# Band scores by halves of the keys, in banks that a run keeps, in a fused two-axis attention layer

## The chip, the cores and the metric

The kernel runs on one core of a Trainium2 chip. The metric is the device time of one execution in microseconds (us), lower being better. The engines of a core are named as the profile names them: PE is the matrix engine (TensorE) and PEld its weight loads, ACT is ScalarE, DVE is VectorE, POOL is GpSimd, and SP is the engine whose queue issues the DMAs. PE writes to PSUM, which has eight banks of 512 fp32 values in each of 128 partitions[...].

## The reference

The input is x of shape [2, 256, 128, 128]: batch, time T, band F, channels C. All of it is fp32. Three residual steps follow each other:

```python
xt = _ln(x, ln_t_w, ln_t_b).transpose(0, 2, 1, 3)
x = x + _mha(xt, ..., H_T, causal mask over T).transpose(0, 2, 1, 3)   # 4 heads of 32 channels
xf = _ln(x, ln_f_w, ln_f_b)
x = x + _mha(xf, ..., H_F, band mask over F)     # |i - j| <= 16 of 128 positions
xn = _ln(x, ln_n_w, ln_n_b)
x = x + (gelu(xn @ w1.T + b1) @ w2.T + b2)       # 128 -> 512 -> 128
```

`_mha` projects to queries, keys and values, takes softmax(q k / sqrt(32) + mask) v for each head, and projects back. What matters here is the second step: for each of the 512 pairs of batch and time there are 128 positions along F, and a position sees only the 33 nearest ones.

## The kernel before

The work is cut into groups of four tiles of 128 tokens (NT = 4), 512 tokens in all. There are three kinds, as classes: `OverTime` (attention along T, 128 groups), `OverBands` (attention along F, 128 groups) and `FeedForward` (128 groups). All groups of time come first; their result goes to HBM and is read back. Then runs follow: 8 groups of bands, then the 8 groups of feed-forward on the same tokens, 16 times (RUN = 32 time steps, `groups`).

`BoundedPath.run` issues the work. Each pass n of its loop issues pieces of several groups: the scores of group n, the weighing by the values of group n - 1, the output product of group n - 2, queries, keys and values of group n + 1, the normalisation of group n + 3, the statistics of groups further ahead. The order is written out by hand: the wrapper `InOrder` pins each engine's instructions to the order in which they are issued, so no scheduler moves them, and all of them carry the wrapper's line (L861) in the profile. The profile is read by the names of the tiles.

A band group goes through these pieces. `queries_keys` computes `qp` and `kp` on PE, and `take_query`, `take_key` copy them by ACT to `qT`, `kT` with channels on partitions. `values` and `take_values` do the same for `vp`, `v`. `scores` (called by `first_half`) computes for each of the 4 tiles and 4 heads the scores `sp`, keys on partitions and queries along the free dimension, a matmul of contraction 32 with 128 keys and 128 queries; every head has a bank, and each head uses its own 32 rows of PE, so four matmuls of one tile can stand side by side. `first_function` lets DVE add a band of -1e30 to the scores of the last head (`band`), and takes four exponentials on ACT into `pf`. `first_mask` lets POOL set what is outside the band to zero for the other three heads, by two selects each. `weigh` computes the row sums `rp` and the weighted values `op` on PE. `invert` takes the reciprocal as exp(-ln) on ACT (`ln`, then `r0`, shown as r), `divide` refines it by one step on DVE (`rp`, `u`) and multiplies `op` by it (`oT`). `output` computes `yp` on PE and `finish` adds it to the residual on DVE (shown as x<-yp). `product` issues a product as four column tiles of 32 where a band or time group is being weighed in the same pass, and as one of 128 otherwise.

The PSUM tiles of the time stage have fixed banks (`Attention.place`, `banks`). The band groups take banks in turn: `turn_of_bank` counts 0 to 7 round and round, over `sp` (four), `yp`, `qp`, `rp`, `op`, `kp` and `vp`; `weigh` takes the turns of `yp` and `qp` ahead of time (`held`). A tile that takes a bank waits until what was in it has been read.

In a pass with band groups on all sides, PE's order is therefore `sp`, `rp`, `op`, `yp`, `qp`, `kp`, `vp`, and ACT's is four exponentials, `ln`, `r`, `qT`, `kT`, `v`. At the turn from bands to feed-forward (`turn` in the code) the last band group is weighed beside the first feed-forward group, and its reciprocal is taken by DVE (`invert_exactly`). `hp` and `zp` are the two products of the feed-forward step, `xh`, `z`, `turned` and `xnT` the normalisation, its transpose, and the way through HBM by which `xnT` arrives with channels on partitions.

Of the kernel before, what the change touches and what calls it, by code (L numbers as in the profile page):

```python
# [10 lines left out]
F32 = mybir.dt.float32  # L11
BF16 = mybir.dt.bfloat16
I32 = mybir.dt.int32
AF = mybir.ActivationFunctionType
# [5 lines left out]
P = 128  # L20
# [404 lines left out]
class Group:  # L425
# [117 lines left out]
    def weigh(self):  # L543
        pass

    def invert(self):
        pass

# [10 lines left out]
class Attention(Group):  # L559
# [8 lines left out]
    def queries_keys(self):  # L568
        path = self.path
        wf = path.k.wf[self.which]  # L570
        self.qp = path.bank([P, NT * P], "qp", self.place.get("qp", path.held.pop("qp", None)))
# [22 lines left out]
    def take_values(self):  # L594
        path = self.path
        self.v = path.work.tile([P, NT, P], F32, name="v", bufs=4)
        path.scalar.copy(self.v, self.vp)

    def invert(self):

        path = self.path
        ln = path.work.tile([P, NT * P], F32, name="ln", bufs=2)
        path.scalar.activation(ln, self.rp, AF.Ln)
        self.r0 = path.work.tile([P, NT * P], F32, name="r0", bufs=2)
        path.scalar.activation(self.r0, ln, AF.Exp, scale=-1.0)

    def invert_exactly(self):
        self.r0 = None
# [17 lines left out]

    def output(self):
        path = self.path
        self.yp = path.bank([P, NT, P], "yp", self.place.get("yp", path.held.pop("yp", None)))
# [115 lines left out]
class OverBands(Attention):  # L745
# [2 lines left out]
    which = 1  # L748
    by_vector = 1

    def scores(self, heads):
        path = self.path
        self.sp = {h: path.bank([P, NT * P], "sp") for h in heads}
        for i in range(NT):
            c = slice(i * P, (i + 1) * P)
            for h in heads:
                r = rows_of(h)
                path.tensor.matmul(self.sp[h][:, c], self.kT[r, c], self.qT[r, c], start=True, stop=True)

    def first_function(self):  # L760
        path = self.path
# [15 lines left out]

    def first_half(self):
        self.p = self.path.work.tile([P, H, NT, P], F32, name="pf", tag="p", bufs=3)
        self.scores(range(H))  # L780

    def weigh(self):
        path = self.path

        path.held = dict(yp=path.turn_of_bank(), qp=path.turn_of_bank())
        self.rp = path.bank([P, NT * P], "rp")
        for h in range(H):
            path.tensor.matmul(
                self.rp[rows_of(h), :], path.k.ones[:, 0:D], self.p[:, h].rearrange("p i q -> p (i q)"),
                start=True, stop=True,  # L790
            )
        self.op = path.bank([P, NT * P], "op")
        for i in range(NT):
            c = slice(i * P, (i + 1) * P)
            for h in range(H):
                r = rows_of(h)
                path.tensor.matmul(self.op[r, c], self.v[:, i, r], self.p[:, h, i, :], start=True, stop=True)


class FeedForward(Group):  # L800
# [34 lines left out]

    def weigh(self):
        path, NI = self.path, self.path.k.NI
        self.zp = path.bank([P, NT, P], "zp")
# [27 lines left out]
class BoundedPath:  # L866
    def __init__(self, ctx, tc, k):
        self.tc, self.nc, self.k = tc, tc.nc, k
        self.xpool = ctx.enter_context(tc.tile_pool(name="xpool", bufs=3))
        self.work = ctx.enter_context(tc.tile_pool(name="work", bufs=3))  # L870
        self.small = ctx.enter_context(tc.tile_pool(name="small", bufs=6))
        self.ps = ctx.enter_context(tc.tile_pool(name="ps", bufs=1, space=PSUM))
        self.next_bank = 0
        self.held = {}
# [12 lines left out]
        for s in (1, -1):  # L887
            tc.nc.gpsimd.affine_select(
                out=self.band, in_=self.band, compare_op=ALU.is_ge, fill=-1e30, base=BAND,
                pattern=[[-s, P]], channel_multiplier=s,  # L890
            )

    def turn_of_bank(self):
        i, self.next_bank = self.next_bank, (self.next_bank + 1) % 8
        return i

    def bank(self, shape, name, i=None):

# [22 lines left out]
    def groups(self, x, out):  # L921
# [33 lines left out]
        for b in range(B):  # L955
            for r0 in range(0, T, RUN):
                run = []
                for t0 in range(r0, r0 + RUN, GB):
                    held = {}


                    def load(g, t0=t0, b=b, held=held):
                        if g == 0:
                            self.quad(held, "x", 4)
                            self.quad(held, "x2", 2 * RUN // GB)
                        self.sync.dma_start(
                            held["x"][rows_of(g)].rearrange("q g t c -> q (g t) c"),
                            self.of_bands(k.x1[b], t0 + NT * g, NT),
                        )

                    def store(g, t0=t0, b=b, held=held):
                        for i in range(NT if g % 2 else 0):
                            self.sync.dma_start(
                                self.of_bands(out[b], t0 + NT * i + g - 1, 2),
                                held["res"][rows_of(i), g - 1 : g + 1].rearrange("q g t c -> q (g t) c"),
                            )

                    def part(name, g, i=None, a=0, held=held):
                        if name == "res" and name not in held:
                            self.quad(held, "res", 2)  # L980
                        if i is not None:
# [4 lines left out]
                for g, part, load, _ in run:  # L986
                    yield OverBands(self, partial(part, "x", g), partial(part, "x2", g), partial(load, g))
# [43 lines left out]
    def run(self, x, out):  # L1031
# [17 lines left out]
        for n in range(-12, len(groups) + 2):  # L1049
# [5 lines left out]
            if bands[2] and feeds[1]:  # L1055
                self.scalar.preload_act_table_set(EXP_SET)
            do_at(n + 4, FeedForward, "root")
            do(n, "first_half", "first_function", "first_mask")
            if old is not None or new is not None:
                time_scores(old, new)  # L1060
                b = self.banks
                Attention.place = dict(rp=b["b0"], op=b["b3"], yp=b["a1"], qp=b["a2"], kp=b["b1"], vp=b["b2"])
            else:
                Attention.place = {}
            if old is not None:
# [5 lines left out]
                old.mask_second()  # L1071
                old.add(0)
            if turn:
                do(n, "second_half", "second_function")
            do_at(n + 3, OverTime, "fetch")
            do_at(n + 2, (OverBands, FeedForward), "fetch")

# [13 lines left out]
                self.fold_rest()  # L1091
                self.warm()
            do(n - 1, "weigh")
            do(n - 1, "invert_exactly" if turn else "invert")
            if new is not None:
                new.first_weights(new.late)
                new.mask_first()
            if old is not None:
                old.add(1)
            if bands[2] or turn or old is not None:  # L1100
                do(n - 2, "output", "finish")
            do(n - 1, "divide")
            if not turn:
# [95 lines left out]
```

## Time and profile before

| | |
|---|---|
| median of 3 runs | 2730.39 us (2729.71 to 2732.25) |
| profiled execution, span | 2727.2 us |
| 32x128 score matmuls of both attentions, 128 queries each | 6144 records, 285 ns mean |
| 32x128 score matmuls with 256 queries (time only) | 2048 records, 388 ns mean |
| exponentials of bands (`pf<-sp`) | 512, 604 ns mean |
| selects of POOL on them | 768, 635 ns mean |
| addition of the band by DVE (`sp<-sp,band`) | 128, 694 ns mean |

An fp32 matmul leaves two records, each a load of weights (PEld) and a matmul (PE). Durations of PE and ACT overlap from one instruction to the next, so a stage is read from where the instructions start, not from the sum of their durations. The granted clock of PE is at full speed from start to end.

The first third of the span (to about 970 us) is the time stage, and the 16 runs of bands and feed-forward follow. In a table by stage, PE is busy without a gap in a stretch of bands (6.44 of 6.44 us, from 1331.00 to 1337.44 us), DVE for 6.30 us of it, ACT for 5.05 and POOL for 4.95. In a stretch of feed-forward (1272.44 to 1279.45 us) PE is busy for 7.01 of 7.01 us and DVE for 3.92.

### The profile page before, as it was taken

The numbers are of one execution on the slowest core, as the hardware profiler recorded it, in microseconds if no ns is written. First come the engines' busy times: TensorE is split into PE (matmuls) and PEld (weight loads), VectorE is DVE, ScalarE is ACT, GpSimd is POOL, SyncE is SP. The second block draws the span as 40 slices with busy tenths as digits, with TensorE's granted clock in tenths as the row PEclk, the third lists the DMA queues.
The fourth block names the chain that finished last, engine by engine and source line by source line (L and its number), as shares of the span: only waits on it lengthen the run. The fifth ranks groups of instructions, "written<-read, shape, count | busy, mean of one in ns | idle before, by whom it ended". The sixth has DMA issues, their size and how long they took to land.

```text
span 2727.2 us, 105787 instructions
## 1 busy us (share of the span) xinstructions
PE 2696.6 (99%) x43538; PEld 1884.4 (69%) x43538; DVE 2280.2 (84%) x6708; ACT 1846.4 (68%) x3620; POOL 1860.8 (68%) x2169
## 2 busy tenths in 40 slices
PE   7999999999999999999999999999999999999998
PEld 5676666666667667676676776766766767767666
DVE  7999999999999987968869779688697796886874
ACT  6888888888888874655745646556556465465563
POOL 3887887887888876666656666666576666665762
PEclk9999999999999999999999999999999999999999
DMA  5555555555555534444444444454454444544533
GB/s 147 146 148 145 147 149 141 148 151 145 142 154 144 134 104 124 114 117 125 110 121 125 108 120 118 117 128 109 120 128 105 121 119 112 133 105 118 133 91 79
DMA packets 471309, 343.83 MB, mean 126 GB/s; under 512 B 43296, under 2 KB 405152, under 8 KB 470816
## 3 DMA queue, kind: packets, MB, share of 16 engines
q1 hardware_dynamic: 469568, 335.92, 48.2%
q8 instruction: 344, 5.64, 0.9%
q14 instruction: 149, 1.22, 0.2%
q10 hardware_dynamic: 1248, 1.05, 0.2%
HBM read 169.03 MB, written 167.77 MB: 123 GB/s over the span
## 4 chain that ended last, share of the span: by engine, by line
PE 73%; DVE 20%; DMA 3%; issue 2%; SPq 1%; POOL 1%; ACT 0%; DVEq 0%; POOLq 0%; ACTq 0%
PE zp L861 17%; PE hp L861 14%; PE sp L861 9%; PE op L861 7%; PE rp L861 6%; PE vp L861 6%; PE qp L861 5%; PE kp L861 5%; PE yp L861 5%; DVE xh L861 4%; DVE stats L861 3%; DVE u L861 2%; DVE rp L861 2%; DVE z L861 2%; DMA xnT<-turned 1%
## 5 line engine op out<-in xcount | busy, mean ns | idle before, releaser
L861 ACT ACTIVATE hT<-hp,b 128x512 f32<-128x512 f32 x512 | 347.7, 687 | 543.6 <-PE hp L861 532.7
L861 POOL TENSOR_SCALAR_AFFINE_SELECT pf<-pf 128x512 f32<-128x512 f32 x768 | 476.9, 635 | 274.3 <-ACT pf L861 248.1
L861 DVE TENSOR_SCALAR xh<-x,mv,rstd 128x160 f32<-128x160 f32 x1536 | 596.7, 430 | 14.2
L861 PEld LDWEIGHTS zp<-w2T_sb,hT 128*128 128x128 f32 x4096 | 476.4, 192 | 56.1 <-issue 54.0
L861 PE MATMUL zp<-w2T_sb,hT 128*128 128x128 f32 x4096 | 479.8, 275 | 0.1
L861 PE MATMUL hp<-xnT,w1f 128*128 128x512 f32 x1024 | 469.2, 596 | 0.0
L861 ACT ACTIVATE p<-sp 128x512 f32<-128x512 f32 (+1 forms) x1024 | 417.2, 500 | 19.8 <-PE sp L861 7.4
L861 POOL TENSOR_SCALAR_AFFINE_SELECT p<-p 128x1024 f32<-128x1024 f32 x256 | 280.1, 1094 | 186.7 <-ACT p L861 186.6
L861 PE MATMUL sp<-qT,kT 32*128 32x128 f32 (+1 forms) x8192 | 362.4, 311 | 5.6 <-DVE oT L861 3.5
L861 PEld LDWEIGHTS sp<-qT,kT 32*128 32x128 f32 x8192 | 310.1, 186 | 56.8 <-ACT kT L861 44.3
L861 PEld LDWEIGHTS vp<-wf,xnT 128*32 128x32 f32 (+1 forms) x7400 | 237.6, 113 | 153.2 <-issue 136.9
L861 POOL TENSOR_TENSOR p<-p,p 128x512 f32<-128x512 f32 x256 | 328.4, 1283 | 10.7
L861 DVE BATCH_NORM_STATS2 stats<-x 128x6 f32<-128x128 f32 x1536 | 326.7, 275 | 0.9 <-DMA x<-in_x 0.9
L861 ACT ACTIVATE pf<-sp 128x512 f32<-128x512 f32 x512 | 264.4, 604 | 59.1 <-PE sp L861 58.9
L861 PEld LDWEIGHTS hp<-xnT,w1f 128*128 128x128 f32 x1024 | 182.2, 191 | 174.6 <-issue 111.0
L861 DVE TENSOR_TENSOR res<-zp,res 128x512 f32<-128x512 f32 x128 | 87.4, 683 | 237.3 <-PE zp L861 237.3
L861 DVE STREAM_TRANSPOSE z<-xh 128x512 f32<-128x512 f32 x384 | 273.2, 711 | 13.2
L861 POOL TENSOR_SCALAR rstd<-mv 128x4 f32<-128x4 f32 x248 | 56.3, 227 | 320.3 <-DVE mv L861 319.3
L861 PE MATMUL vp<-wf,xnT 128*32 128x128 f32 (+1 forms) x7400 | 272.0, 273 | 0.0
L861 PE MATMUL yp<-wn,oT 128*32 128x128 f32 (+1 forms) x7808 | 270.9, 273 | 0.0
L861 POOL TENSOR_TENSOR rstd<-rstd,mhalf 128x4 f32<-128x4 f32 x248 | 256.6, 1035 | 20.7
L861 ACT ACTIVATE qT<-qp,bq 128x512 f32<-128x512 f32 x256 | 176.0, 687 | 136.8 <-PE qp L861 136.8
(92 smaller groups left out, 4214.1 us busy)
## 6 DMA issues: line engine op xcount, KB each, us to landing
turned<-z SPq DMA_DIRECT2D x1536, 64.0 KB, 1.9
xnT<-turned SPq DMA_DIRECT2D x384, 256.0 KB, 3.0
x<-in_x SPq DMA_DIRECT2D x128, 256.0 KB, 4.2
x<-res SPq DMA_DIRECT2D x256, 128.0 KB, 2.4
x<-x SPq DMA_DIRECT2D x128, 256.0 KB, 4.0
out<-res SPq DMA_DIRECT2D x256, 128.0 KB, 2.5
w1T_sb<-in_w1T ACTq DMA_DIRECT2D x1, 256.0 KB, 6.4
w2T_sb<-in_w2T ACTq DMA_DIRECT2D x1, 256.0 KB, 8.3
```

Of the source, the lines that this page charges most:

```text
L861: return self.tc.keep_in_program_order(emit(*args, **kwargs))
```

## The change

The scores of the bands are computed by halves of the keys. For each tile and head there are two matmuls of 64 keys; each takes only the 80 queries that some key of its half can reach (64 + 16). The four banks of scores, 0 to 3, are taken once for a run, and only its first group (`first`) computes whole tiles of 128 by 128; what the later groups don't write keeps old finite scores, which are masked as before. The other tiles of the band stage get fixed places in the other four banks: `rp` (and `zp`) 4, `op` 5, `qp` and `vp` 6, `kp` and `yp` 7; at the turn `rp` has 5 and `op` 6. The bank counter becomes a list that is set anew.

The order in a pass changes: the queries and keys of the next group come right after `weigh`, ahead of the output product, which goes behind the values; the logarithm is a piece of its own, and the query copy stands between it and the second half of the reciprocal. At the turn the first products of the feed-forward step are issued after the places are set.

```diff
 class OverBands(Attention):
+    def scores(self):
+        path = self.path
+        if self.first:
+            path.scored = [path.bank([P, NT * P], "sp", h) for h in range(H)]
+        self.sp = path.scored
+        parts = 1 if self.first else 2
+        n = P // parts
+        reach = P if self.first else n + BAND
         for i in range(NT):
-            c = slice(i * P, (i + 1) * P)
-            for h in heads:
+            for h in range(H):
                 r = rows_of(h)
-                path.tensor.matmul(self.sp[h][:, c], self.kT[r, c], self.qT[r, c], start=True, stop=True)
+                for u in range(parts):
+                    k, q = i * P + u * n, i * P + u * (P - reach)
+                    path.tensor.matmul(
+                        self.sp[h][u * n : (u + 1) * n, q : q + reach], self.kT[r, k : k + n],
+                        self.qT[r, q : q + reach], start=True, stop=True,
+                    )
     def weigh(self):
-        path.held = dict(yp=path.turn_of_bank(), qp=path.turn_of_bank())
-        self.rp = path.bank([P, NT * P], "rp")
+        self.rp = path.bank([P, NT * P], "rp", self.place.get("rp"))
...
-        self.op = path.bank([P, NT * P], "op")
+        self.op = path.bank([P, NT * P], "op", self.place.get("op"))
...
     def run(self, x, out):
-            do(n, "first_half", "first_function", "first_mask")
+            if not turn:
+                do(n, "first_half", "first_function", "first_mask")
...
+            elif bands[2] or turn:
+                Attention.place = dict(rp=5 if turn else 4, op=6 if turn else 5, yp=7, qp=6, kp=7, vp=6)
+                self.turns = list(range(8))
...
             if turn:
-                do(n, "second_half", "second_function")
+                do(n, "first_half", "first_function", "second_half", "second_function")
+                self.turns = [4, 0, 1, 2, 3, 5, 6, 7]
...
             do(n - 1, "weigh")
-            do(n - 1, "invert_exactly" if turn else "invert")
+            if turn:
+                do(n - 1, "invert_exactly")
+            else:
+                do(n - 1, "logarithm")
+                if bands[2]:
+                    do_at(n + 1, OverBands, "queries_keys", "take_query")
+                do(n - 1, "invert")
...
-            if bands[2] or turn or old is not None:
+            if turn or old is not None:
                 do(n - 2, "output", "finish")
             do(n - 1, "divide")
...
-            do_at(n + 1, OverBands, "queries_keys", "take_query", "take_key")
+            if not bands[2]:
+                do_at(n + 1, OverBands, "queries_keys", "take_query")
+            do_at(n + 1, OverBands, "take_key")
...
             do_at(n + 1, OverBands, "values", "take_values")
+            if bands[2]:
+                do(n - 2, "output", "finish")
```

More of the change, by code (lines that the diff above doesn't have):

```diff
@@ L544, in weigh, with logarithm @@
         pass
+    def logarithm(self):
+        pass
     def invert(self):
@@ L570, in queries_keys @@
         wf = path.k.wf[self.which]
-        self.qp = path.bank([P, NT * P], "qp", self.place.get("qp", path.held.pop("qp", None)))
+        self.qp = path.bank([P, NT * P], "qp", self.place.get("qp"))
         product(path, self.qp, wf[:, 0:P], self.xnT)
@@ L597, in take_values, with logarithm @@
         path.scalar.copy(self.v, self.vp)
+    def logarithm(self):
+        path = self.path
+        self.ln = path.work.tile([P, NT * P], F32, name="ln", bufs=2)
+        path.scalar.activation(self.ln, self.rp, AF.Ln)
     def invert(self):
         path = self.path
-        ln = path.work.tile([P, NT * P], F32, name="ln", bufs=2)
-        path.scalar.activation(ln, self.rp, AF.Ln)
         self.r0 = path.work.tile([P, NT * P], F32, name="r0", bufs=2)
-        path.scalar.activation(self.r0, ln, AF.Exp, scale=-1.0)
+        path.scalar.activation(self.r0, self.ln, AF.Exp, scale=-1.0)
     def invert_exactly(self):
@@ L628, in output @@
         path = self.path
-        self.yp = path.bank([P, NT, P], "yp", self.place.get("yp", path.held.pop("yp", None)))
+        self.yp = path.bank([P, NT, P], "yp", self.place.get("yp"))
         for i in range(NT):
@@ L749, with __init__ @@
     by_vector = 1
-    def scores(self, heads):
+    def __init__(self, *args, first):
+        super().__init__(*args)
+        self.first = first
+    def scores(self):
         path = self.path
-        self.sp = {h: path.bank([P, NT * P], "sp") for h in heads}
+        if self.first:
[4 more added lines that the diff above has]
+        reach = P if self.first else n + BAND
         for i in range(NT):
-            c = slice(i * P, (i + 1) * P)
-            for h in heads:
+            for h in range(H):
                 r = rows_of(h)
-                path.tensor.matmul(self.sp[h][:, c], self.kT[r, c], self.qT[r, c], start=True, stop=True)
+                for u in range(parts):
[4 more added lines that the diff above has]
+                    )
     def first_function(self):
@@ L779, in first_half @@
         self.p = self.path.work.tile([P, H, NT, P], F32, name="pf", tag="p", bufs=3)
-        self.scores(range(H))
+        self.scores()
     def weigh(self):
         path = self.path
-        path.held = dict(yp=path.turn_of_bank(), qp=path.turn_of_bank())
-        self.rp = path.bank([P, NT * P], "rp")
+        self.rp = path.bank([P, NT * P], "rp", self.place.get("rp"))
         for h in range(H):
@@ L837, in weigh @@
         path, NI = self.path, self.path.k.NI
-        self.zp = path.bank([P, NT, P], "zp")
+        self.zp = path.bank([P, NT, P], "zp", Attention.place.get("rp"))
         for i in range(NT):
@@ L872, in __init__ @@
         self.ps = ctx.enter_context(tc.tile_pool(name="ps", bufs=1, space=PSUM))
-        self.next_bank = 0
-        self.held = {}
+        self.turns = list(range(8))
         self.banks = dict(zip(("a1", "a2", "b0", "b3", "a0", "a3", "b1", "b2"), range(8)))
@@ L893, in turn_of_bank @@
     def turn_of_bank(self):
-        i, self.next_bank = self.next_bank, (self.next_bank + 1) % 8
-        return i
+        self.turns.append(self.turns.pop(0))
+        return self.turns[-1]
     def bank(self, shape, name, i=None):
@@ L985, in groups @@
                     run += [(g, part, load, store) for g in range(NT)]
-                for g, part, load, _ in run:
-                    yield OverBands(self, partial(part, "x", g), partial(part, "x2", g), partial(load, g))
+                for j, (g, part, load, _) in enumerate(run):
+                    yield OverBands(
+                        self, partial(part, "x", g), partial(part, "x2", g), partial(load, g), first=j == 0
+                    )
                 for g, part, _, store in run:
@@ L1062, in run @@
                 Attention.place = dict(rp=b["b0"], op=b["b3"], yp=b["a1"], qp=b["a2"], kp=b["b1"], vp=b["b2"])
+            elif bands[2] or turn:
+                Attention.place = dict(rp=5 if turn else 4, op=6 if turn else 5, yp=7, qp=6, kp=7, vp=6)
+                self.turns = list(range(8))
             else:
```

## The prediction

> **What bounds the kernel.** I read the page first. TensorE (PE) is busy 99% of the span, but the chain that ended last is PE for only 73% and VectorE (DVE) for 20%.
>
> ```profile
> span 2727.2 us, 105787 instructions
> ...
> PE 2696.6 (99%) x43538; PEld 1884.4 (69%) x43538; DVE 2280.2 (84%) x6708; ACT 1846.4 (68%) x3620; POOL 1860.8 (68%) x2169
> ...
> PE 73%; DVE 20%; DMA 3%; issue 2%; SPq 1%; POOL 1%; ACT 0%; DVEq 0%; POOLq 0%; ACTq 0%
> ```
>
> So a PE at 99% isn't the bound everywhere. Where DVE is, the chain of one run (8 band groups, then 8 feed-forward groups, 108.7 us, 16 times) tells:
>
> ```profile
> 1312.63 1.10 PE sp L861 x32
> ...
> 1318.19 1.12 PE sp L861 x32
> ...
> 1324.64 1.22 PE sp L861 x32
> 1325.96 0.70 DVE sp L861
> 1326.66 1.05 DVE xh L861 x3
> ...
> 1352.08 0.69 DVE sp L861
> ...
> 1357.28 0.70 DVE u L861
> 1358.12 1.07 PE rp L861 x8
> ```
>
> The second, third and fourth score groups (sp) lie on the chain, then it goes over to DVE for 32 us and comes back to PE at the turn, where the last band group's row sums (rp) wait for `u`. In these five iterations DVE also takes the feed-forward statistics, and its period is (1352.08 - 1325.96)/4 = 6.53 us, longer than PE's 6.44. The fifth to eighth score groups are off the chain.
>
> One such iteration in the timeline (start, duration):
>
> ```profile
> 1337.44 1.17 PE L861 MATMUL sp<-qT,kT 32*128 32x128 f32 x32
> 1338.54 1.06 PE L861 MATMUL rp<-pf,ones 128*32 128x512 f32 x8
> 1338.69 2.07 ACT L861 ACTIVATE pf<-sp 128x512 f32<-128x512 f32 x4 [0.53 <-PE sp L861]
> 1341.17 1.04 PE L861 MATMUL qp<-xnT,wf 128*32 128x512 f32 x8
> 1341.28 0.63 ACT L861 ACTIVATE r<-ln 128x512 f32<-128x512 f32 x1
> 1342.33 0.69 ACT L861 ACTIVATE qT<-qp,bq 128x512 f32<-128x512 f32 x1 [0.43 <-PE qp L861]
> 1343.16 0.58 ACT L861 COPY kT<-kp 128x512 f32<-128x512 f32 x1
> 1343.88 1.17 PE L861 MATMUL sp<-qT,kT 32*128 32x128 f32 x32
> ```
>
> A score group holds PE 1.10 us (1337.44 to 1338.54). Last, a wait that the change will multiply; at the start of a run `vp` already waits for `qT`:
>
> ```profile
> 1303.24 0.69 ACT L861 ACTIVATE qT<-qp,bq 128x512 f32<-128x512 f32 x1 [0.17 <-PE qp L861]
> 1303.98 0.97 PEld L861 LDWEIGHTS vp<-wf,xnT 128*128 128x128 f32 x8 [0.75 <-ACT qT L861]
> 1303.99 1.16 PE L861 MATMUL vp<-wf,xnT 128*128 128x128 f32 x8
> ```
>
> From qp's start to the next scores it takes 1305.07 - 1302.19 = 2.88 us there, and 2.70 us (1309.85 to 1312.55) where vp doesn't wait: the wait costs 0.18.
>
> **What the skill says.** The Trainium skill's page Trainium Kernel Development and Optimization, section "Performance Expectations", calls matmul busy time a bad metric of how close a kernel is to the limit, because matmuls are pipelined; here 99% busy stands against 73% of the chain. The skill's page TensorEngine Tiling (Array Packing), "Available Configurations", lists 32x64 tiles as eight independent ones (the scores now use 32x128, four), and "Key Properties" says that a change of mode drains the array: from vp's last matmul to the first score 0.22 us pass, against 0.11 inside a group, so the trace agrees. The skill's page TensorE: Matmul & The Clock Gate, "LDWEIGHTS (loading the stationary operand)", says that a load's time goes with its columns: 187 ns for 128 and 110 for 32 here, 0.8 ns a column. No run here shows 32x64.
>
> **The change, part by part.**
>
> *Scores.* Seven of eight groups issue 32 matmuls of 64 keys x 80 queries for 16 of 128x128 (64 records for 32, as each fp32 matmul leaves two). Now: the first matmul lasts 372 ns against 270, so 0.10 us of weights; the records start in 8 rounds of 4, 0.112 apart; 0.11 of draining: 1.10. A round of 512 columns (rp) takes 0.433, so a column costs 0.84 ns, and 80 columns 0.072. After: 0.05 of weights (64 columns at 0.8 ns) + 8 x 0.072 + 0.11 + 0.03 (eight tiles start 6.7 ns apart instead of four) = S = 0.76. Bounds: 0.60 if the entry and drain hide, 1.10 if the halves of a head don't overlap. I take 0.76.
>
> *Banks and order.* The scores keep banks 0 to 3; qp and vp share bank 6, kp and yp 7, rp has 4, op 5. PE's order becomes sp, rp, op, qp, kp, vp, yp. vp now waits for qT each time, yp for kT; behind them stand only PE's own instructions, so PE loses it in full. On ScalarE (ACT) qT goes ahead of r, so kT comes after r. From a group's start: qp at S + 1.76 (rp 0.88, op 0.87); qT 1.16 later (1341.17 to 1342.33); vp after qT's 0.69 and 0.07, 1.93 after qp instead of 1.72: 0.21 lost. r starts 0.57 after qT, kT 0.54 after r, ends 0.59 later; yp at S + 4.67, then 1.01 to the next scores (0.99 as vp to sp now, 0.02 to fill): S + 5.68 = 6.44. PE before: 6.44. The 0.34 saved is spent on waits.
>
> Other new waits: rp for the last group's u, op for its oT, kp for the last yp's addition: with DVE at most 1.6 us behind its scores, these end before PE gets there. The scores' wait for the previous exponentials is over by 3 us. POOL's masks start with the first exponential, earlier than now, and their 3.9 us had 1.7 to spare. SP's queue and POOL keep their order; ln moved ahead of qT costs nothing, as qT waits for qp (0.43 us idle).
>
> *The chain of a run*, from its first scores:
> - to the second: 7.48 (1305.07 to 1312.55) + 0.18, as vp waits for qT there too
> - to the third (no yp): S + 1.76 + 1.93 + 0.99 = S + 4.68, before 5.58
> - then r of the previous group: S + 1.76 + 1.16 + 0.57 + 0.63 + 0.05 to DVE's rp, and DVE's rp 0.72, u 0.73, oT 0.61, addition 0.58, then the fourth band addition: S + 6.81. DVE waits for r here, which qT has put back.
>
> Sum 19.15 + 2S = 20.67; before, 1325.96 - 1305.07 = 20.89. DVE gains 0.22. From there its work is the same, 32 us without a gap. At the turn rp takes the bank of the previous op, so it waits for oT instead of u: 0.69 + 0.03 more, but the addition of 0.58 has moved behind oT: +0.14. Net -0.08 to -0.12 a run; take -0.11. PE itself would be there 0.5 earlier and waits. The next run starts 55.6 us of PE work later, unchanged.
>
> Over 16 runs: -1.8 us; the profiled execution 2727.2 becomes 2725.4. The three timed runs (2729.71 to 2732.25) have their median 3.2 above that span, so **2728.6**. A single kernel's runs spread by 2.5 us, so I call 0.2%, 5.5 us, what can be told from no change.
>
> The first run after the time stage has the same groups; I add nothing for it.
>
> **Rivals.**
>
> *B, faster: the head of the chain is shorter.* S counts twice in it and a wait may hide. With S = 0.60: 2 x 0.16 = 0.32 a run more, and if the 0.18 at the run's start is hidden too, 0.6 in all: 10 us, 2720. For it: eight tiles may hide each other's entry. Against: the 0.11 drains are seen at every change of mode.
>
> *C, slower: halves of a head don't overlap.* [...] If loads (2 x 0.05) or streams (2 x 0.067) follow each other, a round stays 0.11 and S = 1.10. The bank waits then come on top: period S + 5.68 = 6.78, PE is the bound, and its way to the turn is 7.66 + (S + 4.68) + 5 x (S + 5.68) + S + 6.44 (rp 0.88, op 0.87, yp 0.99, four hp 3.70) = 47.2 + 7S = 54.9, against 53.05: +1.85 a run, +30 us, 2760. It decides from S = 0.85, where PE (53.1) passes DVE; at 0.95 it is +0.8 a run, 2743. For it: no 32x64 in this trace. Against: op runs four column tiles and sp four row tiles side by side at the same 0.11.
>
> *D: PE can't issue fast enough.* The skill's TensorE page, section "Wait — 56ns, not 53.3ns?", has a floor of about 25 ns between matmuls; 64 would take 1.6 us, S 1.75 and 47.2 + 7S = 59.5: +6.4 a run, 2830. The trace has 27 ns a record over whole groups (op: 32 in 0.87 us), but 6.7 ns inside a round; whether PE keeps that up over 64 it doesn't show. It decides from (0.85 - 0.15)/64 = 11 ns a record.
>
> **How the numbers follow.** Forecast 0.40 (its own range 2723 to 2733), B 0.32, C 0.23, D 0.05. Leaving out D, the far half of C and the tip of B gives 2716 to 2744. Faster by over 0.2%: B and 0.01, 0.33; within 0.2%: 0.39; slower: C and D, 0.28.
>
> **What would show it.** Right: a score group of about 0.76; waits of vp for qT and yp for kT, near 0.2 and 0.1 each, 100 times or more; a band period still about 6.44; at the turn PE's rp waiting some 0.5 for oT; DVE gapless over the same stretch; PE's busy share down. Wrong: rounds of 0.11 with eight tiles (C), records 25 ns apart (D), or a fourth band addition well before 20.4 us after the run's first scores (B). A DVE period other than 6.53, or a new wait in the feed-forward groups, would break the sum itself.

## The result, and the profile after

The changed kernel is slower: 2742.24 us median of four runs (2740.95 to 2743.16), against 2730.15 for the kernel before (four runs). The ratio is 1.0042, with a 95% interval of 1.0025 to 1.006. The forecast was 2728.6, no change.

The page of the changed kernel says first that the chain that ended last has moved:

```profile
span 2739.2 us, 113179 instructions
...
PE 2709.4 (99%) x47122; PEld 1860.2 (68%) x47122; DVE 2283.2 (83%) x6708; ACT 1829.1 (67%) x3620; POOL 1860.7 (68%) x2169
...
PE 95%; DVE 3%; DMA 1%; issue 0%; ACT 0%; SPq 0%; DVEq 0%; ACTq 0%
```

PE was busy 99% before and is busy 99% now, but it carries 95% of the chain instead of 73%. The chain of the same run as shown before (start, duration):

```profile
1305.62 1.10 PE sp L881 x32
...
1313.29 0.94 PE sp L881 x53
...
1318.88 0.94 PE sp L881 x55
...
1345.37 0.94 PE sp L881 x55
...
1350.93 1.03 PE yp L881 x32
1351.96 0.68 DVE oT L881
...
1357.76 0.70 DVE u L881
...
1359.39 1.06 PE rp L881 x8
```

Seven of the eight score groups now lie on the chain, each after the first with 0.92 to 1.02 us where 0.76 was forecast. Yet DVE isn't far behind: at the end of the bands the chain goes over to it (from 1351.96), and PE's rp at the turn waits for DVE as before. Both engines are late at nearly the same place. One iteration in the timeline:

```profile
1331.34 0.69 DVE L881 SCALAR_TENSOR_TENSOR u<-rp,r 128x512 f32<-128x512 f32 x1
...
1332.06 1.09 PE L881 MATMUL sp<-qT,kT 32*64 32x80 f32 x64
1332.13 0.69 DVE L881 TENSOR_TENSOR oT<-op,u 128x512 f32<-128x512 f32 x1
1332.74 0.68 DVE L881 TENSOR_TENSOR x<-yp,x 128x512 f32<-128x512 f32 x1
1333.08 1.07 PE L881 MATMUL rp<-pf,ones 128*32 128x512 f32 x8
...
1336.69 0.81 PEld L881 LDWEIGHTS vp<-wf,xnT 128*32 128x32 f32 x32 [0.86 <-ACT qT L881]
...
1337.68 0.81 PEld L881 LDWEIGHTS yp<-wn,oT 128*32 128x32 f32 x32 [0.18 <-ACT kT L881]
```

The group of 64 records holds PE from 1332.06 to 1333.08, 1.02 us. vp waits for qT and yp for kT, as forecast. On DVE, oT starts 0.10 us after u has ended (1331.34 + 0.69 = 1332.03, then 1332.13). In the kernel before that gap was 0.03, and the addition x stood ahead of u:

```profile
1336.39 0.66 DVE L861 TENSOR_TENSOR x<-yp,x 128x512 f32<-128x512 f32 x1
...
1337.69 0.69 DVE L861 SCALAR_TENSOR_TENSOR u<-rp,r 128x512 f32<-128x512 f32 x1
1338.42 0.69 DVE L861 TENSOR_TENSOR oT<-op,u 128x512 f32<-128x512 f32 x1
```

From the traces I took, for every run of 8 + 8 groups but the first, the time from the first scores to the fourth band addition, to the eighth, to rp at the turn, and to the next run's first scores. The medians, with those of five of the kernels below (e3 to e20 are the first letters of their labels):

| kernel | to 4th addition | 4th to 8th | 8th to turn | turn to next run | a run |
|---|---|---|---|---|---|
| before | 20.88 | 26.12 | 6.03 | 55.67 | 108.71 |
| changed | 21.14 | 26.51 | 6.24 | 55.49 | 109.37 |
| e3, S as forecast | 20.91 | 26.43 | 6.24 | 55.49 | 109.06 |
| e9, PE relieved | 21.14 | 26.43 | 6.24 | 55.49 | 109.31 |
| e20, DVE relieved | 21.26 | 26.52 | 6.24 | 55.49 | 109.53 |
| e17, S as forecast, DVE relieved | 21.05 | 25.64 | 6.24 | 55.49 | 108.42 |
| e18, PE and DVE relieved | 20.98 | 25.64 | 6.24 | 55.49 | 108.36 |

The changed kernel's mean run is 109.62, as a few runs are 110.2 to 110.4. 15 x (109.62 - 108.71) = 13.7. The first run, for which the prediction added nothing, takes 1.55 us off that: the second run's first scores come at 1086.11 us, before at 1087.66. That leaves 12.1, and the spans differ by 12.0.

### The profile page after: what moved, and what is told of

It reads as the page before. It is cut to its first block, busy times and chain, and to the rows that moved or that the text cites. A ratio compares the mean times of both kernels' runs of the same rounds, so it can differ in the third digit from the quotient of the medians.

```text
span 2739.2 us, 113179 instructions
## 1 busy us (share of the span) xinstructions
PE 2709.4 (99%) x47122; PEld 1860.2 (68%) x47122; DVE 2283.2 (83%) x6708; ACT 1829.1 (67%) x3620; POOL 1860.7 (68%) x2169
## 3 DMA queue, kind: packets, MB, share of 16 engines
q10 hardware_dynamic: 1248, 1.05, 0.2%
## 4 chain that ended last, share of the span: by engine, by line
PE 95%; DVE 3%; DMA 1%; issue 0%; ACT 0%; SPq 0%; DVEq 0%; ACTq 0%
PE zp L881 17%; PE hp L881 16%; PE sp L881 11%; PE op L881 10%; PE rp L881 9%; PE vp L881 8%; PE yp L881 8%; PE qp L881 8%; PE kp L881 8%; DVE xh L881 1%; DVE stats L881 0%; DVE u L881 0%; DVE rp L881 0%; DVE oT L881 0%; DVE vy L881 0%
## 5 line engine op out<-in xcount | busy, mean ns | idle before, releaser
L881 PEld LDWEIGHTS zp<-w2T_sb,hT 128*128 128x128 f32 x4096 | 476.3, 192 | 56.2 <-issue 54.1
L881 PE MATMUL sp<-qT,kT 32*64 32x80 f32 (+2 forms) x11776 | 348.7, 278 | 6.2 <-DVE u L881 2.3
L881 PEld LDWEIGHTS vp<-wf,xnT 128*32 128x32 f32 (+1 forms) x7400 | 227.5, 113 | 179.6 <-ACT qT L881 95.6
L881 PEld LDWEIGHTS sp<-qT,kT 32*64 32x64 f32 (+1 forms) x11776 | 298.8, 152 | 58.0 <-ACT kT L881 28.0
L881 PE MATMUL qp<-xnT,wf 128*32 128x512 f32 (+1 forms) x1850 | 268.0, 592 | 2.0 <-ACT p L881 2.0
```

Source lines behind the costliest of these rows:

```text
L881: return self.tc.keep_in_program_order(emit(*args, **kwargs))
```

## The experiments

I had three theories. T1: PE isn't supplied with instructions fast enough for 64 short records in a row. T2: the two halves of a head take turns (rival C). T3: the new waits or VectorE, not the scores, make the loss. A ratio is that of a kernel's time to the time of the kernel before in the same session, with its 95% interval.

### What sets the length of a score group

These are the median starts of the 64 records of 105 groups of the changed kernel, in ns from the first:

```
0 7 13 20 27 33 40 47 | 120 127 133 140 147 153 160 167 | 189 196 202 209 216 222 229 236
258 265 272 278 285 292 298 305 | 328
383 397 400 417 459 476 493 501 509 518 534 551 570 576 587 594 604 611 628 644
646 662 679 686 697 703 720 736 753 795 812
```

Four rounds of eight come as forecast: eight tiles 6.7 ns apart, rounds 69 ns apart after the first (which takes 120). So the halves of a head do run side by side, and T2 falls already. After the 33rd record there is a pause of 56 ns, at the same place in nearly every group, and the last 31 come 14 ns apart on average. The record of PE's sequencer at the wait of the next product comes 0.71 us after the group's start (median), when only some eight records are left to start; in e3 below, with 32 records, it comes as early as 0.21 us, with 20 left. That fits a sequencer that hands out the last records just in time.

The Trainium skill's page TensorE: Matmul & The Clock Gate, section "Architectural detail: the array is 16× 32×32, not 1× 128×128", gives PE's queue a depth of 64; if it counts instructions, that is 32 pairs of a weight load and a matmul. The trace fits this: 32 records follow the first one at full pace, and then comes the pause. That the queue is the reason isn't shown by itself; the experiments below show the length of the train. The prediction hadn't used the figure.

**e4_48q** changes only the reach: 48 queries for each half (32 that the band needs are left out), still 64 records.

```diff
-        reach = P if self.first else n + BAND
+        reach = P if self.first else P // 4 + BAND
```

> The changed kernel, with 48 instead of 80 queries for each half of the keys (the other 32 are left out), 64 records as before. If the supply of instructions sets S: the first 33 records start faster, the others as slowly as now, S 0.85 to 1.0 and 2735 to 2743. If the two halves of a head take turns in the stream (rounds of 2 x 0.04): S near 0.83, a run of 108.7, 2729. If the columns streamed set it as the prediction reckoned: S near 0.55 and 2728.

Measured: 2739.84 us, ratio 1.0037 (1.0023 to 1.005). The first 33 records were through in 0.28 us instead of 0.33, the pause came after the 33rd again, the rest came 14 ns apart as before, and a group took 0.92 us (median) instead of 0.99. With 40% fewer columns S lost 7%: beyond the 33rd record the columns don't set the pace.

**e3_lower_keys** issues half the records: it leaves out the upper half of the keys.

```diff
-                for u in range(parts):
+                for u in range(1):
```

> The changed kernel, with only the lower half of the keys scored in seven of eight groups (the upper half is left out): same tiles of 32x64 and 80 columns, but 32 records instead of 64. If PE's supply of instructions sets S (33 records ready, then about 15 ns each): no slow part is left, 8 rounds of 0.072 give S = 0.74, and everything else goes as the prediction had it: period 6.44, VectorE the bound, 2728 to 2730. If a round with 64 keys costs more than its columns for another reason, S stays above 0.85 and the time above 2732.

Measured: 0.71 us for a score group wherever nothing else delayed the next product, close to the forecast's 0.76, with rounds of 0.069 to the end. T1 expected that. But e3 also takes away the second tile of each head, so e14 below has to decide. And the time was 2734.64, ratio 1.0022 (1.0013 to 1.003), not 2728 to 2730: with S as forecast about half of the loss was still there. So a second step of the prediction was wrong too (T3). The timeline of the third group has one part of it:

```profile
1317.20 0.78 PE L881 MATMUL sp<-qT,kT 32*64 32x80 f32 x32
1317.42 0.69 DVE L881 SCALAR_TENSOR_TENSOR u<-rp,r 128x512 f32<-128x512 f32 x1
...
1318.26 1.06 PE L881 MATMUL rp<-pf,ones 128*32 128x512 f32 x8 [0.28 <-DVE u L881]
```

rp's bank is the one that u reads, and a shorter score group brings PE there before DVE has finished.

**e14_two_trains** keeps all 64 records but in two trains of 32, with yp between them: tiles 0 and 1 of the next group go ahead of yp (`first_scores`), tiles 2 and 3 behind it.

```diff
             if bands[2]:
+                do_at(n + 1, OverBands, "first_scores")
                 do(n - 2, "output", "finish")
...
-        self.scores()
+        self.scores((2, 3) if self.early else range(NT))
```

> The changed kernel with the 64 records of a score group in two trains of 32 (query tiles 0 and 1, then yp, then tiles 2 and 3). If the slow half of a score group comes from having more than 33 records in a row that are faster than PE is supplied, both trains go at full pace: 4 rounds of 0.069, 0.42 to 0.47 each, 0.85 to 0.94 together although the array changes its mode twice more, and the irregular groups go. PE's period is then 6.5 to 6.57, VectorE's 6.60 the bound, 2738 to 2741. If every record of this form costs PE about 15 ns wherever it stands, or the third and fourth query tiles are slow for their own reason: second train above 0.55, period 6.7 or more, 2745.

The timeline of one group:

```profile
1332.25 0.53 PE L888 MATMUL sp<-qT,kT 32*64 32x80 f32 x32
1332.72 1.08 PE L888 MATMUL yp<-wn,oT 128*32 128x128 f32 x32
1333.73 0.53 PE L888 MATMUL sp<-qT,kT 32*64 32x80 f32 x32
```

Both trains start all 32 records within 0.305 us and take 0.46, 0.92 together. The same records, with both halves of every head, start at full pace in trains of 32. So the third and fourth query tiles aren't slow for their own reason, nor are eight tiles: it is the length of the train, as T1 has it. That the supply of instructions is what slows a long train is the reading that is left; no run measures the supply itself. The scores' part of the expectation held, the time did not come down: 2743.25, ratio 1.0049 (1.0032 to 1.0066), since PE's period only fell to 6.56 to 6.61 and DVE's is 6.61.

### What the waits cost PE

**e1_full** scores all 128 x 128 in the change's banks and order.

```diff
-        parts = 1 if self.first else 2
+        parts = 1
...
-        reach = P if self.first else n + BAND
+        reach = P
```

> The changed kernel with its banks, order and kept score banks, but every score group in full 128x128 (16 matmuls, 32 records). It asks what the waits for qT and kT cost by themselves. If the formula of the PE path holds (way to the turn 47.2 + 7S, period S + 5.68): S = 1.10, 7.67 from the first scores to the second, then 5.78, then a period of 6.78, a run of 110.6 us against 108.7, a span near 2754 and a time near 2756. If instead the waits cost nothing and the loss of the change sits in the groups of 64 records alone: period 6.44 to 6.5 and 2730.

Measured: 2751.55, ratio 1.0085 (1.007 to 1.0101); PE's period 6.73, a run of 110.11, 0.5 less than I expected. The waits lengthen PE's period by 6.73 - 6.44 = 0.29, where the forecast has 0.34. Halving the scores then won back 0.11 of it (6.62 in the changed kernel).

**e2_nowait** puts vp into the first score bank and yp into bank 6.

```diff
-        self.vp = path.bank([P, NT, P], "vp", self.place.get("vp"))
+        if self.place.get("vp") == "scored" and not self.first:
+            self.vp = path.scored[0].rearrange("p (i c) -> p i c", i=NT)
...
-                Attention.place = dict(rp=5 if turn else 4, op=6 if turn else 5, yp=7, qp=6, kp=7, vp=6)
+                Attention.place = dict(rp=5 if turn else 4, op=6 if turn else 5, yp=7 if turn else 6, qp=6, kp=7, vp=6 if turn else "scored")
```

> The changed kernel with halves of the keys as they are, but vp goes into the first score bank (free after that head's exponential) and yp into bank 6, so vp no longer waits for qT nor yp for kT. If slow second halves of the score groups (S near 1.0) and the two waits are both needed for the loss: PE period S + 5.34 = 6.3 at the longest groups 6.4, DVE is the bound again in the five iterations with statistics, a run of 108.5 to 108.9, time 2727 to 2732. If the groups of 64 records cost the loss alone, wherever they stand: 2740.

Measured: 2752.41, ratio 1.0085 (1.0071 to 1.0098), because the edit brings a wait of its own. From a run's first to its second scores it took 8.23 us instead of 7.67, and 6.18 instead of 5.56 to the third, as the next scores waited for v to leave the score bank. Later in the run PE's period was 6.28 to 6.35, as wanted, and DVE's 6.61. **e9_far** has the same edit, but uses the score bank from the fourth group on only; set against e2:

```diff
-        if self.place.get("vp") == "scored" and not self.first:
+        if self.place.get("vp") == "scored" and self.far:
...
-                        self, partial(part, "x", g), partial(part, "x2", g), partial(load, g), first=j == 0
+                        self, partial(part, "x", g), partial(part, "x2", g), partial(load, g), first=j == 0, far=j >= 3
```

> The changed kernel with halves of the keys as they are; from a run's fourth group on vp goes into the first score bank (free after that head's exponential) and yp into bank 6, so that vp doesn't wait for qT nor yp for kT; the first three groups keep the change's banks (with vp in the score bank from the second group on, the next scores waited for v there, 0.7 us). PE's period should be 6.3 to 6.35 with the same slow scores, VectorE the bound with 6.60: add the way to the fourth band addition of 21.1, 26.42, 6.23 and 55.49: a run of 109.1 to 109.3, 2734 to 2737. If the slow scores alone made the loss: 2742.

Measured: 2740.13, ratio 1.0043 (1.0027 to 1.006). PE's period fell to 6.33 and the two waits were gone from the fourth group on, yet the run is 109.31 instead of 109.37: DVE alone is as slow as the changed kernel. Its band additions come 6.61 apart, 6.53 before. The expected run was right, the expected time 3 us too low.

**e12_after_late** takes DVE's statistics out of one of the five iterations instead.

```diff
-            do_at(n + 4, FeedForward, "root")
+            do_at(n + 3, FeedForward, "root")
...
-            do_at(n + 5, FeedForward, "statistics")
+            do_at(n + 4, FeedForward, "statistics")
```

> The changed kernel with the statistics (and their root) of the feed-forward groups one iteration later, so that four instead of five band iterations of a run carry them: VectorE has 1.05 us less to do on its way to the turn. If PE's period of S + 5.63 = 6.6 is the bound of the changed kernel, as its chain says, nothing moves: a run of 109.4 and 2740 to 2743. If VectorE (period 6.60 there too) is as much the bound, the run gets shorter by up to 0.5 and the time falls to 2734.

Measured: 2744.5, ratio 1.0057 (1.0041 to 1.0074): nothing gained, so PE alone is as slow as the changed kernel as well (e20 below asks this again). Two ways to the turn have both become longer, and shortening one shows nothing.

### VectorE's way

**e10_far_late** joins e9's banks and later statistics; **e8_late_stats** is the control on the kernel before.

> As the kernel with vp in the first score bank from the fourth group on, and with the feed-forward statistics one iteration later too. Both bounds are then lowered: PE's period 6.34, VectorE's 1.05 less in sum. Way to the turn 21.1 + 25.4 + 6.2 = 52.7, a run of 108.2, 2721 to 2724, faster than both kernels. If PE has another wait under VectorE's: 2728 to 2735.

> The kernel before, with the feed-forward statistics one iteration later and nothing else: the control for the other kernels with that edit. VectorE loses 1.05 us on the way to the turn and PE's own period of 6.44 becomes the bound: way 7.48 + 5.58 + 5 x 6.44 + 7.54 = 52.8 against 53.04, 0.24 a run, 2725 to 2727. If VectorE were not the bound of the kernel before: 2729.

Measured: e10 2737.96, ratio 1.0032 (1.0022 to 1.0042), and e8 2726.8, ratio 0.9995 (0.9987 to 1.0004). e10 is 14 us above what I expected. e8's time is within its range, but the interval doesn't tell it from no change, and its run became only 0.10 shorter in the trace (108.61), not 0.24. An iteration without statistics doesn't become 1.05 shorter: it then takes PE's period, 6.34 instead of 6.61 in e10 and 6.44 instead of 6.54 in e8. DVE's period in the other iterations stayed 6.61 and 6.53.

Where do the 0.08 between 6.53 and 6.61 come from? Before, the addition of yp stood ahead of rp, u and oT on DVE, and it had waited for a later product of PE than op. Now it comes last, so oT has two waits, one for u on its own engine and one for op on PE. The Trainium skill's page Perfetto Trace Analysis, section "Identifying Dependency Chains", says that an instruction that waits for several engines may get extra semaphore instructions ahead of it. The trace agrees. In the changed kernel such an instruction stands between u and oT at each of the seven weighings that a run has among its bands, and oT starts 0.104 us after u's end:

```profile
1357.76 0.70 DVE u L881
1358.46 0.03 issue
1358.49 0.02 DVEq L881
1358.51 0.04 issue
1358.56 0.70 DVE oT L881
```

DVEq is VectorE's sequencer, and the 0.02 us are the extra instruction, a wait on a semaphore. In the kernel before it stands there only at a run's first weighing, where no addition goes ahead, with 0.104 again; elsewhere there is none, and oT starts after 0.034. **e13_swap** tests it by putting op ahead of rp on PE, so that DVE's wait for rp covers op.

```diff
     def weigh(self):
+        self.op = path.bank([P, NT * P], "op", self.place.get("op"))
         self.rp = path.bank([P, NT * P], "rp", self.place.get("rp"))
...
-        self.op = path.bank([P, NT * P], "op", self.place.get("op"))
```

> As the kernel with vp in the first score bank from the fourth group on, with op ahead of rp on PE. VectorE's wait for rp then covers op, so oT keeps one wait instead of two and starts 0.03 us after u instead of 0.10. If that second wait is what lengthens VectorE's period from 6.53 to 6.60: 6.53 again, a way to the turn of 53.4 instead of 53.8, a run of 108.9, 2731 to 2734. If the gap has another cause: 6.60 and 2739 to 2741. A rival against the gain: op needs the bank that oT reads last, and PE then waits where it didn't: 2745.

Measured: the extra instruction is gone, oT starts 0.034 after u (median of 120, against 0.104), and DVE's period is 6.54. So the second wait is what lengthened it.

```profile
1333.56 0.70 DVE u L887
1334.26 0.02 issue
1334.28 0.69 DVE oT L887
```

But the time is 2756.31, ratio 1.0101 (1.0084 to 1.0118): the rival named there came true. The chain of e13 at its third group:

```profile
1321.32 0.70 DVE oT L887
1322.02 0.14 issue
1322.15 1.08 PE op L887 x32
```

op now comes first and waits 0.77 us for its bank, which oT reads last: the way to the fourth addition is 21.80 us instead of e9's 21.14. The turn lost 0.5 more, where the chain passes through a load and POOL's addition to res. (rp starts 7.63 us after the last addition instead of 6.24, but 0.87 of that is op ahead of it, and comes back on the way to the next run, 54.62 instead of 55.49.) **e15_all** (e13 with later statistics) and **e16_two_swap** (two trains in the changed kernel's banks) have the same swap.

> Halves of the keys, vp in the first score bank from the fourth group on, op ahead of rp, and the feed-forward statistics one iteration later. PE's period 6.34, VectorE's 6.53 in the iterations with statistics, fewer of which are left: a run of 108.5 to 108.7 and 2725 to 2728, as fast as the kernel before or a little faster. If op's wait for oT holds PE: 2735.

> The changed kernel's banks, with the two trains of 32 score records and op ahead of rp: both causes at once. If PE's supply after 33 records and VectorE's second wait for oT are the two causes, PE's period is 6.5 to 6.57 and VectorE's 6.53: way 53.3 to 53.5, a run of 108.8 to 109.0, 2731 to 2735. If only one of them matters: 2738 or more.

Measured: e15 2753.29, ratio 1.0086 (1.0069 to 1.0103), and e16 2758.36, ratio 1.0106 (1.0089 to 1.0123), the same loss. Neither says anything on the other edits.

### Both causes out of the way

The next kernels leave PE's order alone and put the addition of yp between u and oT, but for the last iteration of a run. **e17_lower_between** has e3's lower half of the keys alone, **e18_far_between** has e9's banks, and **e19_far_late_between** has e9's banks and the later statistics. The edit that they share:

```diff
         vector.scalar_tensor_tensor(u, self.rp, 2.0, self.r0, ALU.subtract, ALU.mult)
+        if between is not None:
+            between()            # finish of group n - 2
         self.oT = path.work.tile([P, NT * P], F32, name="oT", bufs=2)
```

> The kernel with only the lower half of the keys scored (the upper half is left out; 32 records, S 0.71), and in the band iterations the addition of yp between u and oT on VectorE, but for the last iteration of a run. The addition waits for a later product of PE than op, so oT needs no wait of its own for PE. If S and oT's second wait are the two steps of the prediction that failed: VectorE's period 6.53, a run of 108.7 to 108.8, 2728 to 2731. If the second wait doesn't matter: 2734 to 2735.

> Both halves of the keys, vp in the first score bank from the fourth group on, and the addition between u and oT. PE's period is 6.33, VectorE's should be 6.53 instead of 6.61: way 53.8 - 0.35 = 53.45, a run of 108.9 to 109.0, 2733 to 2736. If PE's op now waits for the later oT and hands the loss on: 2739 or more.

> As the one with the addition between u and oT and both halves of the keys, with the feed-forward statistics one iteration later as well: a run of 108.6 to 108.8, 2728 to 2732, level with the kernel before. If PE's op waits for oT: 2736.

Measured: e17 2724.43, ratio 0.9984 (0.9977 to 0.9991); e18 2727.14, ratio 0.9991 (0.9983 to 1.0); e19 2724.35, ratio 0.9984 (0.9977 to 0.999). All three are lower than I expected, for one reason, seen in the timeline of e18:

```profile
1330.76 0.69 DVE L889 SCALAR_TENSOR_TENSOR u<-rp,r 128x512 f32<-128x512 f32 x1
1331.37 0.68 DVE L889 TENSOR_TENSOR x<-yp,x 128x512 f32<-128x512 f32 x1
1331.96 0.68 DVE L889 TENSOR_TENSOR oT<-op,u 128x512 f32<-128x512 f32 x1
1332.56 0.69 DVE L889 TENSOR_TENSOR sp<-sp,band 128x512 f32<-128x512 f32 x1
```

The addition, which doesn't need u, begins 0.08 before u's record ends, and oT 0.09 before the addition's. DVE's period falls from 6.61 to 6.41: 0.07 is the second wait (e13), and the other 0.13 comes from u and oT, which depend on each other, no longer following directly. e19 beats the kernel before by 0.16% and the changed one by more. Its later statistics add nothing that the intervals can tell from e18; the step from e9 (1.0043) to e18 is the addition's place. What the halves bring to e18 isn't shown, as no kernel here scores whole tiles with its banks and order. An estimate from e1: a way to the fourth addition longer by 0.31 (21.45 for 21.14), and a PE period of 6.73 - 0.29 = 6.44 for DVE's 6.41, 0.43 us a run or 7 us in all.

> The changed kernel, with the addition between u and oT, its banks, waits and score groups as they are. VectorE's period would be 6.41, well under PE's 6.63. If PE's way alone is as long as measured (7.67 + 5.57 + 5 x 6.63 + 7.5 = 53.9), nothing is gained: a run of 109.3 and 2740 to 2743. If VectorE was what held the changed kernel: 2727 to 2733.

**e20_after_between** is the changed kernel with this one edit. Measured: 2741.62, ratio 1.0047 (1.0033 to 1.0061), as expected, with a run of 109.53 and a chain that is PE's:

```profile
PE 94%; DVE 4%; DMA 1%; issue 0%; ACT 0%; SPq 0%; DVEq 0%; ACTq 0%
```

With DVE out of the way PE's way alone makes the whole loss, as e9 showed for DVE with PE out of the way.

> The kernel before, with the addition between u and oT instead of ahead of rp: the control. VectorE's period falls from 6.53 to 6.42, under PE's 6.44, so the gain ends at PE: way 52.8 instead of 53.04, a run of 108.5, 2725 to 2727. If the gain is as large as on the kernel with the change (0.2 an iteration): 2714 to 2720.

**e21_before_between**, the kernel before with the addition in the same place, is the control. The expectation was wrong by far: 2780.13, ratio 1.019 (1.0176 to 1.0204). Its waits, from 1300 to 2720 us:

```profile
PEld sp L863 <- DVE x L863: 28.6, 52, 0.9
...
PE sp L863 <- DVE x L863: 18.7, 52, 0.7
```

In the rotation of the kernel before, the next scores take the bank from which the addition reads. A later addition holds them up, and DVE's own band addition then waits 0.76 us for them; its period is 7.26. In the change's fixed banks only kp follows the addition (qp in e18 and e19), and in e17 to e20 no scores wait for the addition. So in these runs the repair of DVE's order paid only together with the change's banks, and in e20, where PE is late too, not even there.

## Why the prediction was wrong

Two steps failed, and either alone makes the kernel slower: with S as forecast e3 still has 1.0022, and with DVE relieved e20 still has 1.0047.

**The size of S.** "8 x 0.072" was right for the first half of a group: 33 records started within 0.328 us. The other 31 took 0.056 + 0.429 to start, and 0.18 passed to rp: 0.99 in place of 0.76. Rival D had the right kind of mechanism, a limit per record, and the wrong size. It set a floor of 25 ns against all 64 records; measured are rounds of eight at 69 ns, 6.7 ns apart inside a round, for the first 33, and 14 ns a record on average for the rest. That is 12.7 ns a record over the whole group (0.81/64), just beyond the 11 ns from which D was to decide, and D had the least chance of all. Rival C had the wrong mechanism, since the halves overlap, but its sum for PE's way, 47.2 + 7S, was good: 54.1 at S = 0.99, 53.9 measured in the changed kernel; 54.9 at 1.10, 54.6 in e1. "At 0.95 it is +0.8 a run, 2743" came close to the result, in part by luck: at the measured 0.99 the sum gives +1.1 a run, about 2748. A saving of 0.18 a run that it doesn't have (below) and the 1.55 us of the first run make 2743 of that.

**"From there its work is the same, 32 us without a gap."** The work is the same but its order isn't: the addition's move behind oT, which the prediction counted at the turn alone (+0.14, measured +0.21), gives oT a second wait in every iteration, which the prediction left out. DVE's period became 6.61 instead of 6.53. Also wrong was that such waits "end before PE gets there": with short scores rp's wait for u cost 0.28 in the third group. Added up for e3: 20.91 - 20.67 = 0.24 at the head, 26.43 - 26.12 = 0.31, and 0.07 at the turn are 0.62 a run beyond the forecast. Against that stands 0.18: vp's wait for qT came at a run's second scores, as forecast (7.67), but the one that the kernel before had at the run's start is gone (55.67 to 55.49), and the prediction had left that stretch unchanged. The net 0.44 over 15 runs is 6.6 us; e3 was 6.0 above the forecast.

**What held:** DVE as the bound of the kernel before (with less work for DVE, e8's run is 0.10 shorter in the trace, though its time can't show so little); the waits of vp and yp, 0.29 together for 0.34; from the first scores to the second 7.67 for 7.66; from the second to the third 5.56 for S + 4.68 = 5.62 at S = 0.94; a period of S + 5.63 for S + 5.68. With both failed steps undone (e17) the kernel took 2724. The repair brought 4 x 0.13 = 0.52 a run more than the wait was worth, 8 us; without that, by this estimate, it would stand near 2732, 3 us above the forecast, with 0.38 at the head (21.05 for 20.67) still on it.

**Left open:** why the queue isn't filled again while its first 33 records start, 0.33 us in which at 14 ns a record some 23 could have come; and the irregular groups (two of 105 last 1.7 and 1.8 us). In the changed kernel the mean run is 0.25 longer than the median, in e1, e3 and e14 at most 0.04. The irregular groups seem to go with the long trains; what makes them was not tried.

## What to carry to other kernels

Count the records that a group issues in a row, not its columns alone: here those after the 33rd ran at 14 ns each whether they had 80 or 48 columns, and a cut of the streamed work was lost there. When an instruction moves behind another on the same engine, look at which waits it had made superfluous for those that it now follows, and whether dependent instructions now stand next to each other. Where two engines are within a per cent or so of each other, take both out of the way before saying which one costs.

## What was new on the hardware

- Matmuls of 32x64 tiles with 80 columns start in rounds of eight, 6.7 ns apart in a round and 69 ns from round to round, for the first 33 records of a train. After a pause of 56 ns the rest start 14 ns apart on average (changed kernel; 14 ns with 48 columns too, e4). Two trains of 32 with another product between them both run at full pace (0.305 us to the last start, e14).
- Where oT waits both for VectorE's own u and for PE, an extra semaphore instruction stands ahead of it and costs 0.07 us, though PE's product has long been there (0.104 against 0.034 us from u to oT; changed kernel against e13).
- VectorE instructions on 128x512 that don't need each other overlap by 0.08 us in the records (e18); one that needs the result before it starts 0.03 after it. An independent one put between two dependent ones gained 0.13 us an iteration (6.54 in e13, 6.41 in e18).
